# One transfer for both halves of a block's rows: fewer, larger loads in a two-layer banded convolution

## The chip, the cores and the metric

The kernel runs on one core of one Trainium2 chip. The metric is the device time of one execution in microseconds (us). The kernel before takes 4308.89 us, the median of three runs (4305.12 to 4312.75). One further execution was taken by the hardware profiler; the traces below come from it.

## What is computed

The input `x` is an image of 512 x 512 positions with 64 channels (f32). Two layers with the same structure follow each other. The reference of a layer, cut to what matters:

```
xn    = layernorm(groupnorm(x))                      # 32 groups of 2 channels over the image; then the 64 channels of a position
left  = (xn @ Wl + bl) * mask * sigmoid(xn @ Wlg + blg)      # 64 -> 128 channels
right = (xn @ Wr + br) * mask * sigmoid(xn @ Wrg + brg)
gate  = sigmoid(xn @ Wog + bog)
out[i, j] = sum over d in -4..4 of left[i+d, i] * right[i+d, j]     # rows i+d that lie in the image, per channel
x     = x + (layernorm(out) * gate) @ Wo + bo
```

So every output row `i` takes the rows `i-4` to `i+4` of `right`, each weighted by one vector per row out of a band along the diagonal of `left`.

## The kernel before, in words

**Blocks and units.** A block is 64 consecutive image rows. Blocks start 56 rows apart, so that neighbours share the rows that the band needs; there are nine, and each gives 56 output rows (60 for the first and the last block, which touch the edge of the image). They are sorted so that the seven with 56 output rows come first. Within a block, the image's 512 columns are cut into a left half and a right half of 256 (`LH`). A **unit** is 8 columns (`JU`) of the left half together with the same 8 columns of the right half: 64 rows of half 0 lie on partitions 0 to 63 and 64 rows of half 1 on partitions 64 to 127. A block has 32 units, so a layer has 288. Eight units make a period.

**What a unit does.** `load` fetches the unit's rows into a tile `z` (128 partitions x 8 columns x 64 channels; a partition's 8 columns are 2 KB that lie together in DRAM). There are 12 such tiles (`NZ`). GpSimd and VectorE apply the group norm and the layer norm to it (`scale`, `move`, `inner`, `centre`, `resc`), TensorE turns it (`ztr`) and multiplies it by the weights of `right` (`proj`), and ScalarE and VectorE gate the result into `RO`. The band product (`mix`, step `band`) multiplies `RO` by slabs of `left`, which lie as banded 64 x 64 matrices in `A`; sixteen units after its `right`, the unit's output is normalized (`norm`), turned, gated, multiplied by `Wo` (`last`), and added to the old rows of `x` (`end`).

**The transfers of a unit.** All of them are issued by SyncE's queue (SP):

- `load` (L514): `z`, two transfers, one for each half, each 64 rows of 2 KB.
- `fetch` (L876): the old rows of `x` to which the output is added, into one of six tiles `XR` (`NX`), two transfers of 56 (or 60) rows. In layer one a row of `XR` has a column of ones on both sides of each pair of positions, for sums that layer two's group norm needs, so that a partition's rows arrive as four pieces of 512 bytes; in layer two they arrive as one piece of 2 KB.
- `stored` (L921): the finished rows from `XR` to DRAM, two transfers with the rows of `fetch`. Layer one writes to `mid_x`, layer two to the kernel's output.
- `take_left` (L706): one of the eight slabs of `A` (16 channels of `left` for 64 rows), four transfers: two halves of the rows by two groups of four channel pairs. A block needs eight slabs for its 32 units, so this is one transfer for each unit on average.

**What sets the order.** The order within a period is written out by hand in two lists, `FIRST` and `SECOND`, one for each layer: a word such as `load:13` means "the load of unit 13 counted from this period's first". Every engine, SP too, carries out its instructions in that order (`en` keeps them in program order), and semaphores make an instruction wait for what it depends on. An SP instruction that waits for something therefore holds up every transfer listed behind it. Before layer one there is a pass over the whole input for the group statistics (16 transfers `gn_x` of 4 MB).

**Lines.** The helper that keeps the order records nearly every instruction under one line (L496), so the profile's groups are told apart by their tiles: `z`, `XR`, `A`, `RO` and so on. `banks`, `bank` and `acc` are PSUM tiles.

Of the kernel before, what the change touches and what calls it, by code (L numbers as in the profile page):

```python
# [20 lines left out]
WIN = 4  # L21
NEAR = 2 * WIN + 1
S = 64
JC = 64
JU = 8
JQ = 4
NU = JC // JU
HA = 16
# [130 lines left out]
def tile_two_banded_layers(  # L159
# [7 lines left out]
    _, L, _, D = x.shape  # L167
    H = layers[0]["Wl"].shape[1]
# [3 lines left out]
    LH = L // 2  # L172
# [15 lines left out]
    span = 2 * (S + 2 * WIN)  # L188
    size = S * H // 2 * span
    left_of = dram.tile([2, size], F32, name="left_of")  # L190
# [86 lines left out]
    def strided(v: bass.AP, at: int, *dims) -> bass.AP:  # L277

        return bass.AP(tensor=v.tensor, offset=v.offset + at, ap=[list(d) for d in dims])


    def fetch_layer(i: int, w: dict, tmp) -> dict:
# [9 lines left out]
        for e in range(2):  # L292
            part = slice(e * D, (e + 1) * D)
            for n, nm in enumerate(("r", "rg", "l", "lg", "og")):
                load(f["raw"][part, n * H : (n + 1) * H], w[f"W{nm}"])
            load(f["ns"][part], col(w["norm_scale"]))
            load(f["nb"][part], col(w["norm_bias"]))
# [207 lines left out]
    class Unit:  # L505
# [4 lines left out]
        def __init__(self, at: int, blk: Block = None, j: int = 0, near: int = None):  # L510
            self.at, self.blk, self.j, self.near = at, blk, j, near
            self.pr, self.sg, self.banks = {}, {}, {}

    def load(src: bass.AP, u: Unit):  # L514
        u.z = zp.tile([P, JU, D], F32, tag=f"z{u.at % NZ}", name="z")
        if u.near is not None:
            load_near(src, u)
            return
        rows = slice(u.blk.s, u.blk.s + S)
        for e, j in enumerate((u.j, LH + u.j)):  # L520
            en.sync.dma_start(u.z[e * S : (e + 1) * S], src[rows, j : j + JU, :])

    def load_near(src: bass.AP, u: Unit):
        spans = [(0, u.near, u.near + JU)]
        if u.near + JU > NEAR * JQ:
            spans = [(o, u.near, u.near + JQ) for o in range(0, JU, JQ)]
        for o0, n0, n1 in spans:
            for o, r, k, m in runs(n0, n1):
                z = u.z[:, o0 + o : o0 + o + m, :].rearrange("q m c -> q (m c)")
                at, q0, q1 = r * (L + 1) + k - WIN, 0, P  # L530
                pieces = []

                if r == 0 and k < WIN:
                    q0, g = 1, min(m, WIN - k)
                    pieces = [(0, 0, g, 0), (0, g, m, at + g)]
                if r == JQ - 1 and k + m > WIN + 1:
                    q1, g = P - 1, max(0, WIN + 1 - k)
                    end = (P - 1) * JQ * (L + 1) + at
                    pieces = [(P - 1, 0, g, end), (P - 1, g, m, L * L - m)]
                cut = [q0, *([16] if q0 else []), *([P - 16] if q1 < P else []), q1]  # L540
                for a0, a1 in sorted(zip(cut, cut[1:]), key=lambda c: c[0] - c[1]):
                    en.sync.dma_start(
                        z[a0:a1],
                        strided(
                            src, (a0 * JQ * (L + 1) + at) * D, (JQ * (L + 1) * D, a1 - a0),
                            (1, m * D),
                        ),
                    )
                for q, g0, g1, a in pieces:
                    if g0 < g1:  # L550
                        en.sync.dma_start(
                            z[q : q + 1, g0 * D : g1 * D],
                            strided(src, a * D, (D, 1), (1, (g1 - g0) * D)),
                        )
# [151 lines left out]
    def take_left(n: int, h: int):  # L706

        held[h] = n
        q = HA // 4
        for e in range(2):  # L710
            for k in range(2):
                en.sync.dma_start(
                    A[e * S : (e + 1) * S, h, k * q : (k + 1) * q].rearrange("p h i t -> p h (i t)"),
                    strided(
                        left_of, n % 2 * size + (h * HA // 2 + k * q) * span + 2 * WIN,
                        (H // 2 * span, S), (span, q), (1, 2 * S),
                    ),
                )

    def mix(c: int, h: int, b: str) -> tuple:  # L720

# [150 lines left out]
    def rows_of(v: bass.AP, o: Out, e: int):  # L872
        b, j = o.blk, e * LH + o.j
        return v[b.s + b.lo : b.s + b.hi, j : j + JU, :].rearrange("p (k t) c -> p k (t c)", t=2)

    def fetch(src: bass.AP, o: Out, n: int, stats: bool):  # L876
        o.xr = XR[n % NX]
        if stats:
            o.f = o.xr[:, :, 1 : 1 + 2 * D]
        else:  # L880
            o.f = o.xr.rearrange("p k c -> p (k c)")[:, : JU * D].rearrange("p (k c) -> p k c", c=2 * D)
        for e in range(2):
            en.sync.dma_start(o.f[e * S : e * S + o.blk.m], rows_of(src, o, e))

# [40 lines left out]
    def layer(src: bass.AP, dst: bass.AP, w: dict, stats: bool, then=None):  # L925
# [51 lines left out]
        def on_load(n, t, alt, b):  # L977
            if slabs:
                take_left(*slabs.pop(0))
            if t in units and t not in early:  # L980
                load(src, units[t])
# [93 lines left out]
        def on_fetch(n, t, alt, b):  # L1075
            if t in outs:
                fetch(src, outs[t], t, stats)
# [10 lines left out]
        def on_band(n, t, alt, b):  # L1088
            if chunk(t):
                c, h = chunk(t)  # L1090
                while held.get(h) != c // per:
                    take_left(*slabs.pop(0))
                mixed[t] = mix(c, h, b)
# [141 lines left out]
    A = keep.tile([P, H // HA, HA // 2, S, 2], F32, name="A")  # L1235
# [38 lines left out]
def build(arrays):  # L1274
    import concourse.bacc as _bacc

    nc = _bacc.Bacc("TRN2", target_bir_lowering=False, num_devices=1)
    aps = {}
    for name in _INS:
        a = arrays[f"in_{name}_dram"]  # L1280
        aps[name] = nc.dram_tensor(
            f"in_{name}_dram", a.shape, mybir.dt.from_np(a.dtype), kind="ExternalInput"
        ).ap()
    out = nc.dram_tensor("out_0_dram", aps["x"].shape, F32, kind="ExternalOutput").ap()
    layers = [{n: aps[f"L{i}_conv_{n}"] for n in _NAMES} for i in range(2)]
    with tile.TileContext(nc) as tc:
        tile_two_banded_layers(tc, aps["x"], layers, out)
    return nc
# [10 lines left out]
```

## Time and profile before

| | |
|---|---|
| Median of three runs | 4308.89 us (4305.12 to 4312.75) |
| The profiled execution | 4288.38 us, of which the span from its first to its last instruction is 4286.6 us |
| Granted TensorE clock | 0.965 |
| TensorE, VectorE, ScalarE, GpSimd busy | 88%, 85%, 74%, 84% of the span |
| Bytes moved by transfers | 596.26 MB, mean 139 GB/s |
| First and last issue of a `z` load, layer one | 166.9 and 2136.8 us |
| First and last issue of a `z` load, layer two | 2211.2 and 4142.7 us |

How to read it: the 16 DMA engines of the core move packets, each a contiguous piece of a transfer. The transfer queue that SP feeds is `q1`; its line gives packets, megabytes, and the time that the packets took as a share of 16 engines' time over the stretch that was asked for. "SPq" is the issuing of a transfer by SP, "PE" TensorE's matmuls, "POOL" GpSimd. A wait such as "POOL z <- DMA z" is idle time of GpSimd ahead of an instruction on a `z` tile, ended by the landing of a transfer.

### The profile page before, as it was taken

How to read it: one execution, taken by the hardware profiler on the slowest of the kernel's cores; microseconds unless marked ns; L12 is line 12 of the kernel's file. 1: busy time of each engine (PE TensorE's matmuls, PEld its weight loads, DVE VectorE, ACT ScalarE, POOL GpSimd, SP SyncE). 2: the span in 40 equal slices, each digit the busy share in tenths (PEclk: the TensorE clock that was granted, in tenths of full speed). 3: DMA queues.
4: the chain of work that ended last, by engine and by line, in shares of the span. 5: the costliest groups of instructions: out<-in, count | busy, mean ns of one | idle time of the engine just before them, and what ended most of it. 6: DMA issues, size and time to landing. Idle time of an engine off the chain costs nothing.

```text
span 4286.6 us, 223301 instructions
## 1 busy us (share of the span) xinstructions
PE 3756.5 (88%) x94986; PEld 3258.3 (76%) x94986; DVE 3657.6 (85%) x9915; ACT 3181.7 (74%) x5976; POOL 3620.0 (84%) x4962
## 2 busy tenths in 40 slices
PE   0169898989899999999995798999999999999998
PEld 0058787878788888888784687878878787878786
DVE  8988787878788888888877798989889898989897
ACT  0048787878787777878773687878888888989896
POOL 2389898989898989999855698998989898989893
PEclk9989999999999999999997899999999999999999
DMA  9843545454545444545434344444454545454533
GB/s 397 318 110 102 140 118 140 114 139 118 142 113 141 122 128 122 136 121 137 129 103 110 97 137 132 136 136 135 132 139 132 141 131 146 128 147 123 157 111 101
DMA packets 695719, 596.26 MB, mean 139 GB/s; under 512 B 138310, under 2 KB 549990, under 8 KB 692420
## 3 DMA queue, kind: packets, MB, share of 16 engines
q1 hardware_dynamic: 692212, 580.43, 47.0%
q8 instruction: 748, 12.26, 1.2%
q14 instruction: 247, 2.02, 0.2%
q0 software_dynamic: 2512, 1.56, 0.1%
HBM read 436.71 MB, written 149.74 MB: 137 GB/s over the span
## 4 chain that ended last, share of the span: by engine, by line
PE 58%; DVE 12%; POOL 9%; DMA 7%; SPq 6%; issue 5%; ACT 2%; DVEq 0%; POOLq 0%; ACTq 0%
PE banks L496 44%; PE bank L496 10%; POOL z L496 6%; SPq L496 6%; POOL on L496 3%; PE acc L496 3%; DVE sti L496 2%; DMA z<-in_x_dram 2%; DVE RO L496 2%; DVE sto L496 2%; DVE gn_st L496 2%; DMA z<-mid_x 2%; DVE XR L496 1%; DVE ZH L496 1%; ACT on L496 1%
## 5 line engine op out<-in xcount | busy, mean ns | idle before, releaser
L496 POOL TENSOR_SCALAR on<-RO,rs,nm 128x128 f32<-128x128 f32 x2520 | 1117.9, 456 | 193.3 <-PE banks L496 139.9
L496 ACT ACTIVATE on<-RO,nm,rs 128x128 f32<-128x128 f32 x2088 | 971.7, 499 | 108.4 <-PE banks L496 95.1
L496 PE MATMUL banks<-pack,ZT 64*128 64x128 f32 x9216 | 987.4, 287 | 24.4 <-DVE RO L496 15.3
L496 PE MATMUL banks<-pack,zT 64*128 64x128 f32 x9216 | 945.0, 279 | 2.2 <-issue 1.3
L496 POOL TENSOR_TENSOR z<-z,ga 128x512 f32<-128x512 f32 x556 | 649.8, 1175 | 301.9 <-DMA z<-in_x_dram 135.3
L496 ACT ACTIVATE sg<-banks 128x512 f32<-128x512 f32 x1170 | 696.1, 596 | 279.9 <-PE banks L496 253.8
L496 PEld LDWEIGHTS banks<-pack,ZT 64*128 64x128 f32 x9216 | 771.5, 194 | 148.4 <-DVE RO L496 49.6
L496 DVE TENSOR_TENSOR RO<-banks,sg 128x512 f32<-128x512 f32 x1152 | 777.6, 683 | 94.8 <-ACT sg L496 72.5
L496 DVE BATCH_NORM_STATS2 sto<-RO 128x6 f32<-128x256 f32 x2304 | 847.9, 413 | 6.7 <-ACT RO L496 2.6
L496 DVE SCALAR_TENSOR_TENSOR ZH<-banks,pack,ZH 128x896 f32<-128x896 f32 (+1 forms) x576 | 668.7, 1161 | 195.5 <-PE banks L496 163.2
L496 PEld LDWEIGHTS banks<-pack,zT 64*128 64x128 f32 x9216 | 754.0, 194 | 3.9 <-ACT zT L496 2.4
L496 PEld LDWEIGHTS banks<-RO,A 64*64 64x64 f32 x36864 | 617.2, 136 | 139.0 <-DVE RO L496 43.9
L496 PE MATMUL banks<-RO,A 64*64 64x64 f32 x36864 | 693.4, 223 | 32.3 <-issue 18.8
L496 PE MATMUL bank<-pack,ZH 128*64 128x64 f32 x18432 | 666.7, 226 | 12.5 <-DVE XR L496 5.6
L496 ACT COPY RO<-banks 128x1024 f32<-128x1024 f32 x540 | 540.2, 1008 | 173.6 <-PE banks L496 162.1
L496 POOL TENSOR_TENSOR z<-z,gb 128x512 f32<-128x512 f32 x556 | 651.5, 1177 | 3.3
L496 PEld LDWEIGHTS bank<-pack,ZH 128*64 128x64 f32 x18432 | 594.0, 139 | 72.9 <-issue 31.0
L496 ACT ACTIVATE ZH<-banks 128x896 f32<-128x896 f32 (+1 forms) x576 | 531.6, 929 | 135.2 <-PE banks L496 129.4
L496 POOL TENSOR_TENSOR z<-z,rs 128x512 f32<-128x512 f32 x586 | 611.9, 1053 | 20.9 <-DVE rs L496 20.5
L496 POOL TENSOR_TENSOR z<-z,sti 128x512 f32<-128x512 f32 x586 | 617.8, 1067 | 7.7 <-DVE sti L496 7.7
L496 PE MATMUL banks<-ZT,pack 64*128 64x448 f32 (+1 forms) x2304 | 587.3, 583 | 3.4 <-issue 1.2
L496 PE MATMUL banks<-ident,on 64*128 64x64 f32 x9216 | 461.7, 230 | 125.7 <-POOL on L496 119.3
(204 smaller groups left out, 4188.7 us busy)
## 6 DMA issues: line engine op xcount, KB each, us to landing
z<-in_x_dram SPq DMA_DIRECT2D x576, 128.0 KB
A<-left_of SPq DMA_DIRECT2D x576, 128.0 KB
z<-mid_x SPq DMA_DIRECT2D x576, 128.0 KB
gn_x<-in_x_dram SPq DMA_DIRECT2D x16, 4096.0 KB
XR<-in_x_dram SPq DMA_DIRECT2D x448, 112.0 KB
mid_x<-XR SPq DMA_DIRECT2D x448, 112.0 KB
XR<-mid_x SPq DMA_DIRECT2D x448, 112.0 KB
out_dram<-XR SPq DMA_DIRECT2D x448, 112.0 KB
```

What stands on the lines that cost most here:

```text
L496: return lambda *a, **k: tc.keep_in_program_order(f(*a, **k))
```

## The change

Three edits, all of them in how a transfer is cut:

- `load`: a `z` tile is filled by one transfer, 128 partitions of 2 KB. The new helper `halves` makes the DRAM side of it: an access pattern of three dimensions, the half (2, stepping 256 columns), the row (64, stepping a whole image row), and the 512 contiguous numbers of a row. The tile's side is 128 partitions of 512 numbers.
- `take_left`: a slab of `A` arrives by two transfers rather than four, one for each half, 64 rows by eight channel pairs of 512 bytes.
- `fetch`, in layer two: one transfer through `halves`, of 64 rows for each half rather than the 56 or 60 that the output needs (the surplus rows are read and not used). It applies where 64 rows from the first output row on lie inside the image: in all blocks but the last, 256 of the 288 units. The last block, `fetch` in layer one, and all stores stay as they were.

```diff
+    def halves(v: bass.AP, j: int) -> bass.AP:
+
+        return v.rearrange("p (e l) c -> e p l c", e=2)[:, :, j : j + JU, :].rearrange(
+            "e p j c -> e p (j c)"
+        )
...
         rows = slice(u.blk.s, u.blk.s + S)
-        for e, j in enumerate((u.j, LH + u.j)):
-            en.sync.dma_start(u.z[e * S : (e + 1) * S], src[rows, j : j + JU, :])
+        en.sync.dma_start(u.z, halves(src[rows], u.j))
...
         held[h] = n
-        q = HA // 4
         for e in range(2):
-            for k in range(2):
-                en.sync.dma_start(
-                    A[e * S : (e + 1) * S, h, k * q : (k + 1) * q].rearrange("p h i t -> p h (i t)"),
-                    strided(
-                        left_of, n % 2 * size + (h * HA // 2 + k * q) * span + 2 * WIN,
-                        (H // 2 * span, S), (span, q), (1, 2 * S),
-                    ),
-                )
+            en.sync.dma_start(
+                A[e * S : (e + 1) * S, h].rearrange("p h i t -> p h (i t)"),
+                strided(
+                    left_of, n % 2 * size + h * HA // 2 * span + 2 * WIN,
+                    (H // 2 * span, S), (span, HA // 2), (1, 2 * S),
+                ),
+            )
...
+        at = o.blk.s + o.blk.lo
+        if not stats and at + S <= L:
+            en.sync.dma_start(o.f, halves(src[at : at + S], o.j))
+            return
         for e in range(2):
             en.sync.dma_start(o.f[e * S : e * S + o.blk.m], rows_of(src, o, e))
```

## The prediction

> **What bounds the kernel now.** I read the page first, then the two layers' steady stretches, 300 to 1900 us and 2350 to 3900 us: waits, the chain, and the transfers in each. The page:
>
> ```profile
> span 4286.6 us, 223301 instructions
> PE 3756.5 (88%) x94986; PEld 3258.3 (76%) x94986; DVE 3657.6 (85%) x9915; ACT 3181.7 (74%) x5976; POOL 3620.0 (84%) x4962
> DMA packets 695719, 596.26 MB, mean 139 GB/s; under 512 B 138310, under 2 KB 549990, under 8 KB 692420
> q1 hardware_dynamic: 692212, 580.43, 47.0%
> z<-in_x_dram SPq DMA_DIRECT2D x576, 128.0 KB
> XR<-mid_x SPq DMA_DIRECT2D x448, 112.0 KB
> XR<-mid_x SPq DMA_DIRECT2D x128, 120.0 KB
> ```
>
> Three engines are busy for 84 to 88% of the span, and the 16 DMA engines for 47%: as the work is cut now, transfers have room. 576 loads of z, two for a unit, make 288 units in a layer. How much SP's queue costs stands in the stretches' chains and waits (layer one's chain, layer two's chain, GpSimd's wait for z in each layer):
>
> ```profile
> by line: PE banks L496 54.5%; PE bank L496 11.7%; PE acc L496 6.6%; POOL z L496 6.2%; DMA z<-in_x_dram 4.7%; issue 4.2%; SPq L496 3.7%; POOL on L496 3.5%; DVE RO L496 0.9%; DVE ZH L496 0.9%; DVE XR L496 0.6%; DVE sto L496 0.4%; DVE sti L496
> by line: PE banks L496 39.7%; PE bank L496 9.6%; SPq L496 9.3%; POOL z L496 8.6%; issue 6.4%; POOL on L496 4.5%; DMA z<-mid_x 3.4%; DVE RO L496 3.0%; DVE sto L496 2.9%; DVE sti L496 2.9%; ACT on L496 1.7%; DVE XR L496 1.6%; ACT RO L496 1.3%
> POOL z L496 <- DMA z<-in_x_dram: 113.3, 36, 6.7
> POOL z L496 <- DMA z<-mid_x: 102.0, 46, 10.8
> ```
>
> SP's issuing is 3.7% of 1600 us in layer one (59 us) and 9.3% of 1550 us in layer two (144 us): that is what fewer transfers can save from. What they can lose is in how a transfer is spread over the DMA engines.
>
> **The pace now.** The transfers issued in each stretch, layer one and then layer two:
>
> ```profile
> q1 hardware_dynamic: 341344, 195.36, 45.8%
> ...
> z<-in_x_dram SPq DMA_DIRECT2D x463, 128.0 KB
> XR<-in_x_dram SPq DMA_DIRECT2D x448, 112.0 KB
> mid_x<-XR SPq DMA_DIRECT2D x444, 112.0 KB
> A<-left_of SPq DMA_DIRECT2D x224, 128.0 KB
> ...
> XR<-in_x_dram SPq DMA_DIRECT2D x6, 120.0 KB
> mid_x<-XR SPq DMA_DIRECT2D x2, 120.0 KB
> ```
> ```profile
> z<-mid_x SPq DMA_DIRECT2D x480, 128.0 KB
> XR<-mid_x SPq DMA_DIRECT2D x448, 112.0 KB
> ...
> XR<-mid_x SPq DMA_DIRECT2D x2, 120.0 KB
> ```
>
> Layer one: 463 z loads are 231.5 units and 454 XR loads are 227; at 229 a unit takes 1600 / 229 = 6.99 us. Layer two: 240 and 225, so 232.5, and 1550 / 232.5 = 6.67 us.
>
> **Over how many engines a transfer is spread.** Two short stretches of layer two hold a few transfers only. From 2828 to 2833 us there are four of 56 rows:
>
> ```profile
> DMA packets 282, 0.48 MB, mean 97 GB/s; under 512 B 56, under 2 KB 56, under 8 KB 280
> q1 hardware_dynamic: 280, 0.46, 28.4%
> out_dram<-XR SPq DMA_DIRECT2D x2, 112.0 KB
> XR<-mid_x SPq DMA_DIRECT2D x2, 112.0 KB
> ```
>
> 280 packets are 4 x 56 = 224 rows of 2 KB and 56 small packets. I read a small packet as the mark with which an engine ends its share: 56 / 4 = 14 engines for 56 rows. From 2820 to 2827.5 us there are four such transfers and two of z, 64 rows each:
>
> ```profile
> DMA packets 442, 0.75 MB, mean 101 GB/s; under 512 B 88, under 2 KB 88, under 8 KB 440
> q1 hardware_dynamic: 440, 0.72, 31.4%
> z<-mid_x SPq DMA_DIRECT2D x2, 128.0 KB
> out_dram<-XR SPq DMA_DIRECT2D x2, 112.0 KB
> XR<-mid_x SPq DMA_DIRECT2D x2, 112.0 KB
> ```
>
> 88 - 4 x 14 = 32, so 16 engines for each z. The number of engines thus divides the count of the outermost dimension: 64 gives 16, 56 gives 14 and not 16. All these transfers have the same outermost count on both sides. The new loads do not: the tile's side counts 128 partitions, the DRAM side counts 2 halves, then 64 rows. [...] So I take it that **the new transfer runs on two engines**, each with 64 packets of 2 KB. The rows cannot show it, since none has unequal sides.
>
> [...]
>
> **The price of a packet.** The nearest rows for a 2 KB packet are z loads by themselves (2834.2 to 2839.6 us), and from below the input pass, with pieces of 32 KB and the engines full (60 to 140 us):
>
> ```profile
> DMA packets 628, 1.05 MB, mean 195 GB/s; under 512 B 121, under 2 KB 121, under 8 KB 627
> q1 hardware_dynamic: 627, 1.04, 61.2%
> z<-mid_x SPq DMA_DIRECT2D x8, 128.0 KB
> ```
> ```profile
> q1 hardware_dynamic: 994, 28.90, 91.6%
> gn_x<-in_x_dram SPq DMA_DIRECT2D x7, 4096.0 KB
> ```
>
> The first: 0.612 x 16 x 5.4 us = 52.9 us of engine time over 627 - 121 = 506 large packets, 0.104 us each (the stretch of 56-row transfers gives 0.284 x 16 x 5 / 224 = 0.101). The second: 0.916 x 16 x 80 = 1172 us for 28.90 MB, which is 0.083 us for each 2 KB. I take 0.086, near the lower end, because in the first price 16 engines read rows a fixed distance apart at the same moment, and two cannot crowd each other so. The bounds are 0.083 and 0.103. A piece of 512 B: layer one's 0.458 x 16 x 1600 = 11,725 us less 463 x 64 z packets at 0.103 (3052) leave 8673 us for (448 + 444) x 56 x 4 + 8 x 60 x 4 + 224 x 256 = 259,072 pieces, 0.034 us with all small packets in it.
>
> **The change part by part.** *Slabs:* two transfers for four, 64 rows outermost on both sides, so 16 engines and the same pieces. They cost nothing; half an issue a unit goes. *z:* the two busiest engines carry 64 packets a unit instead of 4. *Fetch in layer two:* the same for 256 of 288 units, 64 packets instead of 8. Everything else still takes its sixteenth on these two engines too.
>
> Layer one, a unit on each of the two engines: z 64 packets; A 256 / 16 = 16 pieces; XR and store 4 x (56 / 14) x 4 = 64 pieces. So 64 x 0.086 + 80 x 0.034 = 5.50 + 2.72 = 8.22 us against 6.99 now: 1.23 x 288 = +354 us. At 0.083 it is 8.03 (+300), at 0.103 9.31 (+668).
>
> Layer two, 256 units: z 64, fetch 64, stores 2 x 56 / 14 = 8 packets, and A's 16 pieces: 136 x 0.086 + 0.54 = 12.24 us. The last block's 32 units keep the two fetches (60 rows, 4 packets on an engine each) and have 64 + 8 + 8 = 80 packets: 7.42 us. Together 256 x 12.24 + 32 x 7.42 = 3371 us against 288 x 6.67 = 1921: +1450 us. At 0.083 it is 3259 (+1338), at 0.103 4006 (+2085).
>
> The two engines then set the pace; all else lies beside them: the compute of a unit (at most 6.99 us) and SP, which is spared 1.5 of 7 issues a unit in layer one and 2.5 in layer two. The twelve z tiles keep several loads listed ahead, so I count no gaps. [...]
>
> Sum against the profiled execution's 4288.38 us: 4288 + 354 + 1450 = 6092. The median of the runs is 20.5 us above that execution, so **6110 us**; with the bounds 5950 and 7060.
>
> **The rivals.** *A, all 16 engines carry it:* decided by whether the split follows the tile's 128 partitions. For it: 64 / 16 and 56 / 14 are also four partitions to an engine. [...] Then the packets stay spread and only issues go: 59 x 1.5 / 7 = 13 us and 144 x 2.5 / 7 = 51 us, for 288 units rather than 229 and 232.5 together 80 us. GpSimd's 36 + 46 waits for z may each shorten by one issue:
>
> ```profile
> L496 SPq DMA_DIRECT2D z<-mid_x x592: 215/595/2077, 2211.2 to 4142.7; - x198
> ```
>
> 82 x 0.595 = 49 us, 61 for whole layers, part of which PE, next in the chain at over 49%, would keep. I price A at -80 us: 4230, faster. *B, two engines, but hidden:* needs a packet under (6.67 - 0.54) / 136 = 0.045 us, half the lowest price in the trace. The 80 us saved then stand against 82 waits for z that last some 2 us longer (64 x 0.045 = 2.9 us for a transfer, against 4 x 0.103 for a share and an issue), 205 us for whole layers: about 4430.
>
> **How the numbers follow.** Two engines at the rows' prices: 0.88. A: 0.09. B: 0.03. A change within 0.2% (8.6 us) is about what a measurement of this kernel cannot tell from none. Faster 0.08 (A, nearly whole), slower 0.90, the same 0.02. The range is that of the likeliest case, which alone holds over 8 in 10. Its lower end has layer one's cost hidden and a packet at 0.078, an estimate that takes 5% of crowding out of the 0.083: 256 x 11.15 + 32 x 6.78 = 3071, so 4309 + 1150 = 5460. Its upper end is 7060 with 2% for moments in which the two engines' queue runs empty: 7200.
>
> **What would show it.** The packets under 512 B count engines. z: 576 x 2 for 1152 x 16, 17,280 fewer; slabs 288 x 16 fewer, 4608; fetch 256 x 2 for 448 x 14 + 64 x 15, 6720 fewer: 138,310 becomes about 109,700. If A holds it is about 121,000 (9216, 4608 and 3136 fewer). The DMA row falls to 2 or 3 tenths in layer two, since two engines of 16 are full; GpSimd's waits for z grow from 102 us to over 1000, with PE, VectorE and GpSimd under 65% busy in layer two; layer one's z loads span some 2300 us and layer two's some 3400. The forecast is wrong if the small packets say 121,000, or if they say 109,700 and waits for z do not lead the table; wrong in size if a z packet costs more than 0.103 us, or the two engines stand idle because SP is held behind a store.

## The result and the profile after

The changed kernel takes 6494.56 us (median of four runs, 6492.35 to 6500.17) against 4310.82 us for the kernel before: a ratio of 1.506, 95% interval 1.5021 to 1.5099. The forecast was 6110 us in a range of 5460 to 7200. The direction and the main mechanism came out as forecast; the size was 385 us short. The profiled execution took 6500.17 us; that of the kernel before took 4288.38 us, 17 us less than the fastest of its timed runs, so differences between the two profiles come out a little larger than those between medians.

The page of the changed kernel, in the lines that answer to those shown of before:

```profile
span 6498.4 us, 221512 instructions
PE 4262.4 (66%) x94986; PEld 3656.2 (56%) x94986; DVE 3699.7 (57%) x9915; ACT 3205.0 (49%) x5976; POOL 3622.7 (56%) x4962
...
DMA  9423243333333342432222222222312222221222
...
DMA packets 670939, 603.91 MB, mean 93 GB/s; under 512 B 109702, under 2 KB 521382, under 8 KB 667652
...
q1 hardware_dynamic: 667444, 588.18, 30.1%
```

GpSimd, VectorE and ScalarE do nearly the same work as before (GpSimd 3620 us before, 3623 after); what has grown is the time between. TensorE's busy time did grow, from 3757 to 4262 us, while its granted clock was 0.818 rather than 0.965; it is nevertheless idle for a third of the span. The small packets are 109,702; two engines for each merged transfer meant "about 109,700", sixteen "about 121,000". And the DMA row shows 2 and 3 tenths in a kernel whose longest waits are for transfers: a mean over sixteen engines hides two that are full.

One can see them directly in a short stretch of layer one (1563 to 1575 us, 40 slices of 0.3 us; the first row is the busy share of all 16 engines in tenths, the second the rate):

```profile
DMA  1111111111111000058741968211221111111111
GB/s 48 48 55 48 48 48 48 48 55 48 39 44 39 7 0 0 2 118 254 230 135 27 265 164 248 84 36 24 70 75 44 55 55 55 41 55 55 55 41 55
```

Where mostly z packets are left the row says 1 tenth, as two busy engines of sixteen give, and the first ten slices move 48 to 55 GB/s together, some 25 GB/s for each engine. After thirteen such slices stand four with next to nothing (7, 0, 0 and 2 GB/s): the two engines ran empty. SP's issues around that gap (start and duration in us):

```profile
1554.38 0.53 SPq L496 DMA_DIRECT2D z<-in_x_dram  x1
1554.96 4.70 SPq L496 DMA_DIRECT2D mid_x<-XR  x2
1567.14 0.78 SPq L496 DMA_DIRECT2D XR<-in_x_dram  x2
1568.03 0.53 SPq L496 DMA_DIRECT2D z<-in_x_dram  x1
```

SP issued a z load and two stores, and then, for all but 0.1 us of the time up to 1567.14, waited for a store to `mid_x` to land. In the trace the last 64 packets of the stores (512 bytes; 16 for each of the two stores in each of two streams) come behind those of z, from 1566.1 to 1567.0 us; SP goes on right then, and no packet is under way until 1568.1. This pattern comes back below.

The waits that lead the table, first over the whole execution, then SP's own, and then GpSimd's and SP's before the change:

```profile
POOL z L496 <- DMA z<-mid_x: 1577.3, 168, 23.3
...
POOL z L496 <- DMA z<-in_x_dram: 839.7, 165, 15.4
...
DVE XR L496 <- DMA XR<-mid_x: 672.4, 55, 33.2
```
```profile
SPq L496 <- DMA mid_x<-XR: 698.1, 139, 7.9
SPq L496 <- DVE XR L496: 554.4, 117, 12.5
SPq L496 <- DMA out_dram<-XR: 436.5, 65, 8.7
```
```profile
POOL z L496 <- DMA z<-in_x_dram: 135.3, 44, 6.7
POOL z L496 <- DMA z<-mid_x: 114.5, 52, 10.8
```
```profile
SPq L496 <- DMA mid_x<-XR: 207.2, 137, 3.6
```

GpSimd's waits for z were 135 us in layer one and 114 us in layer two; they are 840 and 1577 us now. SP's wait for stores to layer one's `mid_x` to land has grown from 207 to 698 us: as in the stretch above, a store's share on the two engines stands behind the z packets there.

How long the z loads of each layer take from first to last issue shows where the time came from (the last two numbers of a row before the semicolon; layer one before, then layer one and layer two of the changed kernel):

```profile
L496 SPq DMA_DIRECT2D z<-in_x_dram x592: 246/588/1962, 166.9 to 2136.8; - x198
```
```profile
L496 SPq DMA_DIRECT2D z<-in_x_dram x304: 246/534/7397, 167.5 to 2839.9; - x152
L496 SPq DMA_DIRECT2D z<-mid_x x304: 214/3273/7793, 2919.9 to 6339.3; - x152
```

Layer one's z loads span 2672 us against 1970 before (+702), layer two's 3419 against 1931 (+1488). Together 2190 of the 2212 us that lie between the two profiled executions. The issue of a z load in layer two has grown from 595 to 3273 ns (the middle one of three durations): SP now spends time inside the issue itself, which no semaphore wait shows.

### The profile page after: what moved, and what is told of

Its sections match the earlier page's. It is cut to its first block, busy times and chain, and to the rows that moved or that the text cites. A ratio compares the mean times of both kernels' runs of the same rounds, so it can differ in the third digit from the quotient of the medians.

```text
span 6498.4 us, 221512 instructions
## 1 busy us (share of the span) xinstructions
PE 4262.4 (66%) x94986; PEld 3656.2 (56%) x94986; DVE 3699.7 (57%) x9915; ACT 3205.0 (49%) x5976; POOL 3622.7 (56%) x4962
## 2 busy tenths in 40 slices
DMA packets 670939, 603.91 MB, mean 93 GB/s; under 512 B 109702, under 2 KB 521382, under 8 KB 667652
## 4 chain that ended last, share of the span: by engine, by line
PE 23%; POOL 21%; issue 20%; DMA 20%; SPq 9%; DVE 5%; ACT 1%; POOLq 0%; DVEq 0%; ACTq 0%
PE banks L496 18%; POOL z L496 13%; SPq L496 9%; DMA z<-mid_x 9%; POOL on L496 8%; DMA z<-in_x_dram 7%; PE bank L496 4%; PE acc L496 2%; DVE gn_st L496 1%; DMA XR<-mid_x 1%; DVE ZH L496 1%; DVE RO L496 0%; DVE XR L496 0%; DMA mid_x<-XR 0%; DMA XR<-in_x_dram 0%
## 5 line engine op out<-in xcount | busy, mean ns | idle before, releaser
L496 PE MATMUL banks<-pack,ZT 64*128 64x128 f32 x9216 | 1117.1, 315 | 267.1 <-DVE RO L496 258.7
L496 PE MATMUL banks<-ident,on 64*128 64x64 f32 x9216 | 573.4, 252 | 1006.9 <-POOL on L496 1000.5
L496 PEld LDWEIGHTS banks<-pack,ZT 64*128 64x128 f32 x9216 | 888.0, 219 | 613.6 <-DVE RO L496 283.4
L496 DVE TENSOR_TENSOR XR<-bank,XR 120x512 f32<-120x512 f32 (+1 forms) x576 | 393.3, 683 | 1286.5 <-DMA XR<-mid_x 672.4
L496 PEld LDWEIGHTS banks<-ident,on 64*128 64x128 f32 x9216 | 451.7, 157 | 1138.5 <-POOL on L496 1081.5
L496 PE MATMUL banks<-pack,zT 64*128 64x128 f32 x9216 | 1054.6, 302 | 2.7 <-issue 1.7
L496 PEld LDWEIGHTS banks<-pack,zT 64*128 64x128 f32 x9216 | 867.2, 218 | 2.7 <-ACT zT L496 2.3
L496 DVE BATCH_NORM_STATS2 sti<-z 128x6 f32<-128x128 f32 x2344 | 505.7, 282 | 538.5 <-POOL z L496 537.8
L496 PE MATMUL bank<-pack,ZH 128*64 128x64 f32 x18432 | 765.5, 245 | 31.9 <-DVE XR L496 24.9
L496 ACT ACTIVATE ZT<-banks 128x512 f32<-128x512 f32 x576 | 342.4, 594 | 824.8 <-PE banks L496 824.7
```

Source lines behind the costliest of these rows:

```text
L496: return lambda *a, **k: tc.keep_in_program_order(f(*a, **k))
```

## The experiments

Each ratio is to the kernel before as it ran on the same chip, where its median lay between 4319 and 4328 us. Where no ratio is given, the kernel was executed once; the executions of the kernel before differ by some 20 us among themselves, and smaller differences should not be read. The layers' z spans are those of the profiled executions.

**z alone.** The edit of `load`, with its helper `halves`, without the others:

```diff
-        for e, j in enumerate((u.j, LH + u.j)):
-            en.sync.dma_start(u.z[e * S : (e + 1) * S], src[rows, j : j + JU, :])
+        en.sync.dma_start(u.z, halves(src[rows], u.j))
```

> Only z is loaded by one transfer; slabs and fetch as before. Theory (two engines carry each merged transfer and set the pace): layer one is as in the changed kernel, its z loads spanning about 2670 us against 1970 before (+700 us); layer two has 64 + 8 + 8 = 80 large packets a unit on each of the two engines, 7.4 us against 6.67 now, +210 us if they never run empty and up to +500 if they run empty as often as in layer one. Together 5200 to 5500 us. Rival (each merged transfer costs a fixed time wherever it stands, 2184 us over 832 merged transfers, 2.6 us each): 576 of them, +1510 us, 5820 us. Packets under 512 B: 138,310 - 17,280 = 121,030 by the theory.

```profile
DMA packets 678432, 596.13 MB, mean 102 GB/s; under 512 B 121031, under 2 KB 532711, under 8 KB 675141
...
L496 SPq DMA_DIRECT2D z<-mid_x x304: 214/509/5587, 2948.3 to 5665.8; - x152
```

Measured: 5827.27 us against 4322.45, +1505 us. The small packets (121,031) agree with two engines. The time does not agree with the theory's 5200 to 5500: it is the rival's figure. Layer one behaves as in the changed kernel (z span 2700 us); layer two's z span is 2718 us, +786 where +210 to +500 was expected. By this run alone a fixed cost for each merged transfer would stand.

**fetch alone**, the early return in `fetch`, with `halves`, without the others:

```diff
+        at = o.blk.s + o.blk.lo
+        if not stats and at + S <= L:
+            en.sync.dma_start(o.f, halves(src[at : at + S], o.j))
+            return
```

> Only layer two's fetch is one transfer; z and slabs as before. Theory (two engines): layer one unchanged; layer two has 4 + 4 + 64 + 8 = 80 large packets a unit on each of the two engines, 7.4 us against 6.67, so +190 to +450 us, 4500 to 4760 us; so z alone and fetch alone together cost clearly less than the 2184 us of the whole change, because layer two is loaded past its pace only by both. Rival (a fixed 2.6 us for each merged transfer): 256 of them, +670 us, 4980 us, and the two parts add up to the whole. Packets under 512 B: 138,310 - 6,720 = 131,590 by the theory.

Measured: 4742.63 us, +420 us, inside the theory's range and below the rival's; the small packets are the expected 131,590. In layer two z alone added 786 us and fetch alone 432 (z span 2363 us); both together added 1488. A fixed price for each transfer would add up to 1218. That both together cost more fits two loads on the same two engines, where the spare room that each alone still finds can be used only once.

**Slabs alone**, the edit of `take_left`:

> Only the slabs come by two transfers instead of four; 64 rows stay outermost on both sides. Theory: still 16 engines each, half an issue a unit less: 0 to -20 us. Rival (merging as such costs): 288 transfers fewer but each dearer, some +100 us or more.

Measured: 4255.89 us, ratio 0.9844 (0.9824 to 0.9863), 66 us faster: more than the 20 expected. What the profiles show of the gain lies in layer one:

```profile
L496 SPq DMA_DIRECT2D z<-in_x_dram x592: 230/589/1777, 167.6 to 2086.7; - x198
L496 SPq DMA_DIRECT2D z<-mid_x x592: 215/595/1972, 2161.7 to 4108.1; - x198
```

Layer one's z loads span 1919 us against 1970, layer two's 1946 against 1931; the two profiled executions differ by 35 us, so about half of the 66 us is not located. In the stretch from 300 to 1900 us, GpSimd's waits for z fell from 113.3 to 63.8 us, and SP's share of the chain from 3.7% to 1.1%. Slabs are taken at the `load` steps, ahead of the z load, so four issues became two just there. That this place is why the gain was larger than expected is likely, but was not tested.

**The same transfers with 128 rows outermost.** In the changed kernel's `halves`:

```diff
-        return v.rearrange("p (e l) c -> e p l c", e=2)[:, :, j : j + JU, :].rearrange(
-            "e p j c -> e p (j c)"
+        return v.rearrange("p (e l) c -> (p e) l c", e=2)[:, j : j + JU, :].rearrange(
+            "r j c -> r (j c)"
         )
```

> The whole change, but the DRAM side of each merged transfer counts 128 rows in one dimension (row by row, both halves of a row next to each other), so that the halves lie interleaved on the partitions and the numbers are not the reference's. Same number of transfers, of packets and of bytes as the changed kernel. Theory (the outermost count of 2 decides): 16 engines again, and 4230 us, 80 us under the kernel before; packets under 512 B 121,350. Rival (one large transfer in place of two, or the surplus rows, are what costs): 6400 us or more.

```profile
DMA packets 682587, 603.96 MB, mean 141 GB/s; under 512 B 121350, under 2 KB 533030, under 8 KB 679300
```

Measured: 4270.96 us, ratio 0.9874 (0.9859 to 0.9889), 51 us faster than the kernel before, and 41 us above the 4230 expected. Same number of transfers as in the changed kernel, same bytes, same surplus rows; only the order of the dimensions differs, and the small packets are 121,350, as sixteen engines give. This run takes the loss away whole: merging is not what cost. That it is no faster than slabs alone (4255.89 us) says that the merged z and fetch, even on sixteen engines, bring nothing beyond the slabs.

**Four engines.** The 128 rows cut 4 x 32, so that the slowest dimension counts 4:

```diff
-            "r j c -> r (j c)"
+            "(i n) j c -> n i (j c)", n=4
```

> As the run with 128 rows in one dimension, but those rows are cut so that the slowest dimension counts 4 (4 x 32; rows land on other partitions than the reference's). Theory (engines = slowest count): four engines share the merged transfers. Layer two: 32 + 32 + 8 = 72 large packets a unit on each of the four, 72 x 0.086 + 0.54 = 6.7 us against some 6.6 now; layer one 32 x 0.086 + 2.72 = 5.5 us, hidden. So 4270 us if the four never run empty, up to 4600 us with gaps as in layer one of the changed kernel: most of the 2184 us goes with two engines becoming four. Small packets 109,702 + 832 x 2 = 111,366. Rival (anything but a plain list of rows is dear): 6000 us or more.

```profile
DMA packets 672604, 603.92 MB, mean 125 GB/s; under 512 B 111367, under 2 KB 523047, under 8 KB 669317
...
L496 SPq DMA_DIRECT2D z<-mid_x x304: 215/530/5410, 2376.9 to 4686.7; - x152
```

Measured: 4840.01 us, with 111,367 small packets. Three quarters of the loss go with two engines becoming four, but 240 us more stay than the range allowed for. Layer two took 2310 us (8.0 us a unit) where 6.7 us of packets a unit were counted. Part of that is gaps: from 2500 to 4500 us the trace has fewer than four packets under way for 11% of the time, some 0.9 us a unit.

**Two engines without merging.** The kernel before, its two transfers kept, each half's rows cut in two:

```diff
-            en.sync.dma_start(u.z[e * S : (e + 1) * S], src[rows, j : j + JU, :])
+            en.sync.dma_start(u.z[e * S : (e + 1) * S], src[rows, j : j + JU, :].rearrange("(i n) j c -> n i (j c)", n=2))
...
-            en.sync.dma_start(o.f[e * S : e * S + o.blk.m], rows_of(src, o, e))
+            of = rows_of(src, o, e)
+            if not stats:
+                of = of.rearrange("(i n) k c -> n i (k c)", n=2)
+            en.sync.dma_start(o.f[e * S : e * S + o.blk.m], of)
```

> The kernel before with its two transfers for z and, in layer two, two of 56 or 60 rows for fetch, slabs as before, but each half's rows cut 2 x 32 (2 x 28, 2 x 30), so that the slowest dimension counts 2 with nothing merged (rows land on other partitions than the reference's). Theory: two engines carry them as in the changed kernel, layer two with 64 + 56 + 8 = 128 large packets a unit, 11.6 us, layer one as changed: 6200 to 6500 us. Rival (the merging costs, not the spread): 4310 us.

Measured: 6427.62 us against 4323.12. Nothing is merged, no surplus row is read, and nearly the whole loss is there:

```profile
DMA packets 672551, 596.17 MB, mean 93 GB/s; under 512 B 115142, under 2 KB 526822, under 8 KB 669252
...
L496 SPq DMA_DIRECT2D z<-in_x_dram x592: 229/529/5895, 167.3 to 2895.8; - x198
L496 SPq DMA_DIRECT2D z<-mid_x x592: 215/1414/7357, 2976.5 to 6243.4; - x198
```

115,142 is what two engines give for each of these transfers: 138,310 less 1152 x 14 for z and less 448 x 12 + 128 x 13 for fetch. With the run of 128 rows, this settles the cause: a count of two in the slowest dimension of the DRAM side, with or without a merge.

**Eight XR tiles**, against the gaps of layer one, in the changed kernel:

```diff
-NX = 6
+NX = 8
```

> The changed kernel with eight XR tiles instead of six. It asks why layer one takes 9.4 us a unit where the two engines' packets make up some 8.2 to 8.7. Theory A: SP, held until a store has landed before it may reload that XR tile (636 us of waits in 2300 us of layer one), lists the next z loads too late, and the two engines run empty; with two more tiles the wait goes and layer one loses 150 to 350 us: 6150 to 6350 us. Theory B: packets are dearer than the 0.086 us taken and the engines are full: no more than 40 us less. Layer two, where they are full, stays at 12.0 us a unit by both.

Measured: 6285.75 us, 209 us less. SP's waits in layer one, from 400 to 2500 us (the changed kernel had 636.2 us in "DMA mid_x<-XR" from 400 to 2700 us), and the issues there:

```profile
SPq L496 <- DVE XR L496: 309.8, 53, 9.9
SPq L496 <- PE banks L496: 289.8, 125, 5.0
SPq L496 <- DMA z<-in_x_dram: 112.8, 73, 3.3
...
z<-in_x_dram SPq DMA_DIRECT2D x243, 256.0 KB
```

The wait for landing stores is gone from the head of the table, and a unit takes 2100 / 243 = 8.64 us. Layer two stays as it was: z span 3414 us against 3419. This is what theory A expected.

**Fifteen z tiles, loads listed earlier**, in the changed kernel:

```diff
-NZ = 12
+NZ = 15
...
-last:-1 sig1:-1 move:4 sums:-3 scale:10 right0:-1 stp:-2 norm7:0 load:11 keep0:0 ost2:6 gate:0@0
+last:-1 sig1:-1 move:4 sums:-3 scale:10 right0:-1 stp:-2 norm7:0 load:14 keep0:0 ost2:6 gate:0@0
```

and so every `load` word in both lists.

> The changed kernel with fifteen z tiles instead of twelve and every z load listed three units earlier. Theory C: the z loads are listed too close ahead of their use, so that in layer one GpSimd's wait for z and SP's waits hand the lateness to and fro and the two engines run empty; with three units more lead layer one loses 150 to 350 us: 6150 to 6350 us. Theory B (the engines are full): no more than 40 us less. Theory A (SP held by landing stores, wherever the loads stand): no more than 100 us less.

Measured: 6314.08 us, 180 us less, all in layer one (z span 2495 us); layer two's is 3414 us. This is what theory C expected. From 400 to 2500 us SP still waits 642.5 us for landing stores (580.5 us in the changed kernel), yet the loads are listed far enough ahead. So theory B, that the engines are full in layer one, falls with both runs, and either remedy closes much of the gap: what lacked was enough loads in the queue ahead of SP's next hold. The packets of the traces, counted by how many are under way at a moment, say the same. In the changed kernel fewer than two are under way for 11% of the time from 400 to 2700 us (254 us), with either remedy for 6% from 400 to 2500 us. In layer two, from 3300 to 6100 us, it is 0.2%. The two remedies together were not run.

**Half the z transfers with sixteen engines.** On top of the slabs, one transfer loads one half of two neighbouring units, so 64 rows of 4 KB (fourteen z tiles in pairs, loads listed two units earlier):

```diff
-            en.sync.dma_start(u.z[e * S : (e + 1) * S], src[rows, j : j + JU, :])
+            en.sync.dma_start(
+                z[e * S : (e + 1) * S].rearrange("p u j c -> p (u j) c"),
+                src[rows, j : j + 2 * JU, :],
+            )
```

> Half the z transfers with all 16 engines kept: slabs by two transfers, and a transfer loads one half of two neighbouring units, 64 rows of 4 KB, 64 outermost on both sides (fourteen z tiles in seven pairs, loads listed two units earlier). Theory (the spread costs, fewer issues are worth little once the slabs are halved): 4220 to 4260 us, at most 35 us under slabs alone (4256 us). Rival (each saved issue is worth its 0.6 us while SP is in the chain): 288 issues a layer less, 4100 to 4180 us. Packets under 512 B: 133,702 - 9,216 = 124,486.

Measured: 4258.92 us, ratio 0.9866 (0.9843 to 0.9889), small packets 124,486. Nothing beyond slabs alone. But the run changes two things at once, the number of issues and the lead of the loads. GpSimd's waits for layer one's z have fallen to 3.8 us in it, and why the time did not follow is open.

**Slabs with fifteen z tiles**, the two edits shown above together.

> Slabs by two transfers, z and fetch as before, fifteen z tiles and z loads listed three units earlier. If the waits for z that are left (64 us in 1600 us of layer one, 90 us in 1550 us of layer two with slabs alone) are lateness of listing: 4150 to 4220 us. If PE is the next bound: 4230 to 4260 us.

Measured: 4211.15 us, ratio 0.9737 (0.972 to 0.9754), the fastest kernel here: 2.6% under the kernel before, and inside the range for loads that were listed late. GpSimd's waits for z, 250 us in both layers together before, are 9.7 us in layer two, and for layer one they have left the table of the longest waits.

**Slabs with eight XR tiles.**

> Slabs by two transfers, z and fetch as before, eight XR tiles instead of six. SP waits some 186 us in 1600 us of layer one for stores to land before it reloads an XR tile; with 16 engines this holds nothing up that is late: 4235 to 4260 us. If it does hold z loads back as in the changed kernel: 4150 to 4220 us.

Measured: 4220.03 us, ratio 0.9772 (0.9754 to 0.9789), at the upper end of the second case. Its waits for z are 60.3 us in layer one and 111.6 in layer two, against 81.7 and 110.8 with slabs alone, so z loads that come earlier explain at most a part of the 36 us between the two; SP's waits for layer one's stores, 238 us with slabs alone, have left the head of its table. What else it did is left open.

**Eight engines.** The 128 rows cut 8 x 16.

> As the run with 128 rows in one dimension, but with the rows cut so that the slowest dimension counts 8 (8 x 16; rows land on other partitions than the reference's). Theory: eight engines, layer two 16 + 16 + 8 = 40 large packets a unit on each, 40 x 0.10 + 0.54 = 4.5 us, well under the pace of 6.6 us, so nearly all of the loss is gone: 4270 us (as with 16 engines) to 4350 us. With four engines the packets were near the pace (7.7 us at 0.10) and 4840 us was measured. If a loss of over 150 us stays, bursts on few engines cost even where the mean load leaves room. Small packets: 111,366 + 832 x 4 = 114,694.

```profile
DMA packets 675931, 603.93 MB, mean 138 GB/s; under 512 B 114694, under 2 KB 526374, under 8 KB 672644
...
L496 SPq DMA_DIRECT2D z<-in_x_dram x304: 229/621/3111, 167.3 to 2157.1; - x152
L496 SPq DMA_DIRECT2D z<-mid_x x304: 215/577/2813, 2232.9 to 4231.4; - x152
```

Measured: 4409.95 us, ratio 1.0193 (1.0176 to 1.021), 60 us over the range. The series in full, as the z spans of both layers: two engines 2672 and 3419 us, four 2134 and 2310, eight 1990 and 1999 (in the fastest of its five executions, 4378.40 us), sixteen 1934 and 1947. By the medians eight engines still cost 139 us over sixteen, where their counted load in layer two is two thirds of the pace and fewer than eight packets are under way for 37% of the time (2350 to 4100 us): they are not full. GpSimd's waits for z are 142.7 and 185.4 us with eight, 77.9 and 94.4 with sixteen: a z tile that takes longer to fill arrives late more often. That is the likely path; it was not tested by itself.

## Why the prediction was right, and where it was short

**The two engines: right.** The step was from the rows of before, whose outermost counts of 64 and 56 gave 16 and 14 engines, to a DRAM side that counts 2. Those rows could not show it, their two sides being equal; the counts of small packets now do, to within one, for outermost counts of 2, 4, 8 and 128 on the DRAM side (109,702, 111,367, 114,694 and 121,350). The changed kernel's 109,702 is exactly what the prediction's sum gives before rounding. The sums of both layers also rest on one pair of engines that carries z, fetch and a share of every store. The rows of before did not show that; the changed kernel's trace does. From 3300 to 6100 us, where merged loads of both kinds are queued, just two packets are under way for 64% of the time; and the last 64 packets of two stores, from 1566.1 to 1567.0 us, come behind z packets in just two streams. One transfer of 128 partitions did no harm where its DRAM side counts the rows in one dimension (4270.96 us); with the two halves outermost it took 6494.56 us.

**Layer two: right in size.** The changed kernel's issues from 3300 to 6100 us:

```profile
z<-mid_x SPq DMA_DIRECT2D x233, 256.0 KB
XR<-mid_x SPq DMA_DIRECT2D x232, 256.0 KB
```
```profile
q1 hardware_dynamic: 183431, 206.76, 23.1%
```

A unit takes 2800 / 232.5 = 12.04 us; 12.24 was forecast, and the layer's z span grew by 1488 us for a forecast of 1450. With full engines a large packet costs (12.04 - 0.54) / 136 = 0.085 us on them, beside the 0.086 taken. That they are full agrees with the two runs that closed gaps in layer one and left this layer as it was, and with the 0.2% of the time in which fewer than two packets are under way. So the lower TensorE clock cannot be what holds this layer back. The choice of a price near the lower end is borne out too: in layer two a packet of 2 KB takes 90 ns in the mean with two engines, 95 with four, 104 with eight and 109 with 128 rows outermost, and 84 ns in the middle in all four. That this is engines crowding each other, the reason given, no run tests.

**Layer one: the step that failed** is "The twelve z tiles keep several loads listed ahead, so I count no gaps". From 400 to 2700 us:

```profile
z<-in_x_dram SPq DMA_DIRECT2D x244, 256.0 KB
...
XR<-in_x_dram SPq DMA_DIRECT2D x442, 112.0 KB
...
XR<-in_x_dram SPq DMA_DIRECT2D x42, 120.0 KB
```

244 and 242 units in 2300 us are 9.47 us a unit, where 8.22 us of packets were counted: 1.25 x 288 = 360 us, nearly all of the 385 us that the forecast was short. The packets were not mis-sized by so much, since with eight XR tiles a unit takes 8.64 us with the same packets. The engines ran empty in between, for 11% of the time or 1.0 us a unit by the count of packets under way: SP may not reload an XR tile before its store has landed, the store's share stands behind z packets on the two engines, and while SP waits, the next z loads stay unlisted. The prediction named this as a thing that would make it wrong in size ("the two engines stand idle because SP is held behind a store") but gave it only 2%, at the upper end. That the total stayed inside the range is owed to the range: its upper part was there for a dearer packet, and gaps filled it. Gaps were also underrated in the expectation for z alone in layer two (9.4 us a unit against 7.4): there fewer than two packets are under way for 13% of the time from 3000 to 5500 us, 1.3 us a unit. Of the signs that the prediction named, this layer's z span alone did not come: 2672 us, where some 2300 were forecast. One slip is without effect: 5% off 0.083 is 0.079 and not 0.078, which puts the lower end at some 5500 us.

**The slabs: the sign right, the size not.** "They cost nothing; half an issue a unit goes" left out where the issues stand, ahead of a z load; the gain was 66 us, though no run shows that the place is the reason. **The rivals:** A was priced at 80 us for all saved issues; the kernel that does what A supposes gained 51 us, no more than the slabs alone. B needed packets of 0.045 us, and they cost 0.085.

## What to carry to other kernels

Before halves or groups are merged into one transfer, look at the slowest dimension of the DRAM side: in the runs here its counts of 2, 4, 8, 56, 60, 64 and 128 went with 2, 4, 8, 14, 15, 16 and 16 engines by the count of small packets, and the same 256 KB went over two engines or sixteen. None of the changed transfers has the smaller count on its tile side. A mean DMA share of 23% hid two full engines. A mean load below the pace was no cover either: eight engines at two thirds of the pace cost 139 us, perhaps because each load takes longer to arrive. As for saving issues, two slab issues fewer and three units more lead gave 2.6% together, while merging z and fetch on sixteen engines gave nothing beyond the slabs.

## What was not expected of the hardware

Issuing itself took long: in the changed kernel's layer two, where the two engines are full, SP's issue of a z load took 3273 ns in the middle and up to 7793 ns, against 595 ns in the middle before. Its layer one's XR loads, of 56 or 60 rows, took up to 7382 ns, against 1982 before. With two engines without merging, layer two's z loads took 1414 ns in the middle, with 128 rows outermost 418. No run shows what holds SP there, and the table of SP's waits does not contain the time. TensorE's granted clock was 0.818 in the changed kernel against 0.965, in a kernel whose TensorE was busy 66% rather than 88% of the span; a matmul `banks<-pack,ZT` took 315 ns in the mean against 287. The other runs with long waits for z have a lower clock too (0.858 with z alone, 0.822 with two engines without merging, against 0.972 with 128 rows outermost), so it goes with the waits; no run here separates its cause.
